# A sort loop on one core: the ranks in pieces between the products, the target rows in three parts, weights and zeros issued from inside the loop

## The chip, the cores and the metric

The kernel runs on one core of a Trainium2 chip. The metric is the device time of one execution in microseconds (us). The kernel before was run 14 times: median 19117.52 us, lowest 19084.45, highest 19168.0. The core has a matrix engine (PE), a vector engine (DVE), a scalar engine (ACT), GpSimd (POOL) and SyncE (SP), which here issues transfers (DMAs). Each runs its own list of instructions in order, and they meet at semaphores.

## The reference

A graph with 12500 nodes (16 features each) and 412500 directed edges, the edges ordered by `dst`, passes through four graph layers, each added to `x`. What the changed part of the kernel does is the edge half of layer 0, for all edges:

```
h   = maximum(layernorm(x), 0)
x_j = h[dst]                                             # 412500 rows
m   = silu(einsum('ei,ej,ijh->eh', x_j, edge_attr_8, W_msg_tp) / sqrt(16 * 8))
m   = m @ W_msg_lin / sqrt(16)
agg = segment_sum(m, src, num_segments=12500)
...                                                      # node update, then x = x + ...
```

Layers 1 to 3 (a weighted message layer, an encoder with two edge and node blocks, two graph convolutions) use the same edges in the order into which layer 0's stage has sorted them. Of them only the loading of their weights is touched.

## The kernel before

The nodes are padded to 12544 = 98 windows of 128 (`ND`). The edges of a window (by `dst`) lie together in the input, so a window is a stretch of 35 x 128 edge records (`TL` = 35) of 16 words. Within its window every edge gets a slot by the group of its source node: a table of 37 x 128 slots (`TT` = 37; the last 5 of the 37 columns take what overflows), kept in DRAM as `cells`. From the slots, messages can be computed with one-hot matrix products and without address lists.

**Before the loop.** `tile_gnn` first builds constants, then loads all weights of the four layers with SP and prepares them on DVE: L188 to L288, with the helpers `load_w` (L114), `load_b` (L119), `center` (L124), `pair_diag` (L131), `bias_rows` (L144) and `twice` (L232). SP then loads `X`, and ten DMAs from one large tile of zeros (L322 to L327) clear the sum tables in DRAM. `relu_ln` (L729, called at L1600) forms H = relu(layernorm(X)), and `table128` (L988) forms a table `t_msg` of 128 numbers for each node. `sort_edges` (L366) begins with `window_starts` (L335), which counts on DVE where each window's edges begin; a sum over partitions on POOL ends it.

**The loop** (L413 to L466) runs 98 + 5 times; an iteration serves windows of different age. It is written under a manual schedule for PE, DVE, ACT and SP: the engines' lists have the order of the program text. The pieces of the `Window` class (L478), with the age at which a window meets them:

- `load` (age -1; SP): clears the window's slots in DRAM and loads its edge records `rec`.
- `keys` (age 0; DVE, L498 to L513): source group of each edge. `hot_cells` (L516, L518): the one-hot rows `s_ohs` of these groups, 128 x 4480 numbers. `count` (L520 to L527; PE): 36 matmuls that count edges by group.
- `look_up` (age 1; DVE): ten small operations from the counts (L535 to L545), then one multiply (L547) and one reduction (L548) over 128 x 4480 numbers, then `s_eq`, the comparison of all edges of a partition with one another in two parts (L554 to L558). `rank` (L561 to L593): 25 small operations that end in `s_row`, the row of each edge in the table. `scatter` (L595; POOL): 35 indirect DMAs (L597) of 128 records each.
- `read_back` (age 3; SP): loads the window's slots as `c`. `slot_rows` (age 3; PE L613, ACT L615 and L616): transposes the slot numbers and writes them to `slot_lo`.
- `load_rows` (age 4; SP, L618 to L622): loads `u` from `slot_lo` and `win` from `t_msg`. `hot_rows` (age 4; ACT, L624 to L632): the one-hot rows `hot_dt` of the target nodes in three parts (`PARTS`: 16, 16 and 5 columns; three buffers).
- age 5 (`old`): `gather(i)` (PE, L641), for ten chunks (`CHUNKS`, nine of 4 columns and one of 1), one-hot matmuls into one of two PSUM banks `pl`, two records in the profile for each matmul; `products(i)` (DVE, L650), their product with the edge features; `message(i)` (DVE L662, ACT), the reduction of a part of the columns and silu; `hot_sources` (DVE, L656), one-hot rows of the source nodes; `to_sources` (PE, L675), 32 matmuls (64 records) that add the messages into the accumulators `acc`.

PE, DVE and POOL are bound together: `rank` follows on `count` of the iteration before, `scatter` on `rank`, `products` on `gather`, and `gather(i + 2)` must wait for `products(i)`, because there are two `pl` banks. `slot_rows` takes a `pl` bank too. In the code before, an iteration issues, after the loads, `look_up`, `rank` and `scatter` of the window of age 1 first, and then the gathers, products and the rest in the order of the text printed here.

Of the kernel before, what the change touches and what calls it, by code (L numbers as in the profile page):

```python
# [11 lines left out]
F32 = mybir.dt.float32  # L12
# [35 lines left out]
def tile_gnn(ctx: ExitStack, tc: tile.TileContext, a: dict, out: bass.AP):  # L48
# [82 lines left out]
    def pair_diag(name, src, centered):  # L131

        d = consts.tile([P, P], F32, name=name)
        two = consts.tile([P, 64], F32, name=name + "_2")
        v.memset(d, 0.0)
        sp.dma_start(two[0:64, :], src)
        sp.dma_start(two[64:128, :], src)
        if centered:
            center(two, 64)
        v.tensor_copy(d[0:64, 0:64], two[0:64, :])  # L140
        v.tensor_copy(d[64:128, 64:128], two[64:128, :])
        return d

    def bias_rows(name, src, centered):  # L144

        b = consts.tile([3, 64], F32, name=name + "_f")
        sp.dma_start(b, row_bc(src, 64, 3))
        if centered:
            center(b, 64)
        part = consts.tile([3, 3, 64], BF16, name=name + "_p")  # L150
        back = consts.tile([3, 64], F32, name=name + "_b")
        acc = consts.tile([3, 64], F32, name=name + "_a")
        for k in range(3):
            v.tensor_copy(part[:, k, :], b)
            v.tensor_copy(back, part[:, k, :])
            v.tensor_sub(b, b, back)
            if k == 0:
                v.tensor_scalar(acc, back, ident[0:3, 0:1], None, op0=ALU.mult)
            else:
                v.scalar_tensor_tensor(acc, back, ident[0:3, k:k + 1], acc, op0=ALU.mult, op1=ALU.add)  # L160
        r = consts.tile([P, 8, 64], BF16, name=name)
        v.memset(r, 0.0)
        v.tensor_copy(r[0:3], acc[:, None, :].to_broadcast([3, 8, 64]))
        return r.rearrange("p t f -> p (t f)")
# [27 lines left out]
    wml = load_w("wml", a["L0_gnn_W_msg_lin"], 16, 16)  # L192
    v.tensor_scalar(wml, wml, 0.25, None, op0=ALU.mult)
    wupd = load_w("wupd", a["L0_gnn_W_upd_tp"].rearrange("i h k -> i (h k)"), 16, 256)
    v.tensor_scalar(wupd, wupd, 1.0 / 16.0, None, op0=ALU.mult)
    wul = load_w("wul", a["L0_gnn_W_upd_lin"], 16, 16)
    v.tensor_scalar(wul, wul, 0.25, None, op0=ALU.mult)
    w1t = load_w("w1t", a["L1_w_iao"], 16, 128)
    w1c = consts.tile([P, 16], F32, name="w1c")
    for j in range(8):  # L200
        sp.dma_start(w1c[16 * j:16 * j + 16, :], a["L1_w_iao"][:, 16 * j:16 * j + 16])
    b1_l1 = load_b("b1_l1", a["L1_gnn_bias"], 16)

    p2 = "L2_gnn_"
    ne_w0 = load_w("ne_w0", a[p2 + "node_enc_w0"], 16, 64)
    ne_b0 = load_b("ne_b0", a[p2 + "node_enc_b0"], 64)
    ne_w1 = load_w("ne_w1", a[p2 + "node_enc_w1"], 64, 64)
    center(ne_w1, 64)
    ne_b1 = load_b("ne_b1", a[p2 + "node_enc_b1"], 64)
    center(ne_b1, 64)  # L210
    ne_g = load_b("ne_g", a[p2 + "node_enc_g"], 64)
    ne_be = load_b("ne_be", a[p2 + "node_enc_beta"], 64)

    ee_w0 = consts.tile([P, 8, 64], F32, name="ee_w0")
    v.memset(ee_w0, 0.0)
    for t in range(TS):
        sp.dma_start(ee_w0[8 * t:8 * t + 8, t % 8, :], a[p2 + "edge_enc_w0"])
    ee_w0 = ee_w0.rearrange("p t f -> p (t f)")

    ec_w0 = consts.tile([P, 8, 64], F32, name="ec_w0")  # L220
    v.memset(ec_w0, 0.0)
    for t in range(8):
        sp.dma_start(ec_w0[WORDS * t:WORDS * t + 8, t, :], a[p2 + "edge_enc_w0"])
        sp.dma_start(ec_w0[WORDS * t + W_ONE:WORDS * t + W_ONE + 1, t, :], row_bc(a[p2 + "edge_enc_b0"], 64, 1))
    ec_w0 = ec_w0.rearrange("p t f -> p (t f)")
    ee_b0 = bias_rows("ee_b0", a[p2 + "edge_enc_b0"], False)
    ee_w1 = pair_diag("ee_w1", a[p2 + "edge_enc_w1"], True)
    ee_b1 = bias_rows("ee_b1", a[p2 + "edge_enc_b1"], True)
    ee_g = load_b("ee_g", a[p2 + "edge_enc_g"], 64)
    ee_be = load_b("ee_be", a[p2 + "edge_enc_beta"], 64)  # L230
# [8 lines left out]
    ee_g2 = twice("ee_g2", a[p2 + "edge_enc_g"])  # L239
    ee_be2 = twice("ee_be2", a[p2 + "edge_enc_beta"])  # L240

    eb, nb = [], []
    for s in range(2):
        w0, f = a[p2 + "edge_blk_w0"][s], {}
        f["w0e"] = pair_diag(f"eb_w0e{s}", w0[0:64, :], False)
        f["w0sd"] = consts.tile([64, 128], F32, name=f"eb_w0sd{s}")
        sp.dma_start(f["w0sd"][:, 0:64], w0[64:128, :])
        sp.dma_start(f["w0sd"][:, 64:128], w0[128:192, :])
        f["b0"] = load_b(f"eb_b0{s}", a[p2 + "edge_blk_b0"][s], 64)
        f["w1"] = pair_diag(f"eb_w1{s}", a[p2 + "edge_blk_w1"][s], True)  # L250
        f["w1x"] = consts.tile([P, P], F32, name=f"eb_w1x{s}")
        v.memset(f["w1x"], 0.0)
        sp.dma_start(f["w1x"][0:64, 64:128], f["w1"][64:128, 64:128])
        sp.dma_start(f["w1x"][64:128, 0:64], f["w1"][0:64, 0:64])
        f["b1"] = bias_rows(f"eb_b1{s}", a[p2 + "edge_blk_b1"][s], True)
        f["g"] = load_b(f"eb_g{s}", a[p2 + "edge_blk_g"][s], 64)
        f["be"] = load_b(f"eb_be{s}", a[p2 + "edge_blk_beta"][s], 64)
        f["g2"] = twice(f"eb_g2{s}", a[p2 + "edge_blk_g"][s])
        eb.append(f)
        f = {}  # L260
        f["w0"] = load_w(f"nb_w0{s}", a[p2 + "node_blk_w0"][s], 128, 64)
        f["b0"] = load_b(f"nb_b0{s}", a[p2 + "node_blk_b0"][s], 64)
        f["w1"] = load_w(f"nb_w1{s}", a[p2 + "node_blk_w1"][s], 64, 64)
        center(f["w1"], 64)
        f["b1"] = load_b(f"nb_b1{s}", a[p2 + "node_blk_b1"][s], 64)
        center(f["b1"], 64)
        f["g"] = load_b(f"nb_g{s}", a[p2 + "node_blk_g"][s], 64)
        f["be"] = load_b(f"nb_be{s}", a[p2 + "node_blk_beta"][s], 64)
        nb.append(f)

    eb[0]["sum_be"], eb[1]["sum_be"] = consts.tile([P, 64], F32, name="sum_be"), eb[1]["be"]
    v.tensor_add(eb[0]["sum_be"], eb[0]["be"], ee_be)

    be0 = twice("eb_be2", a[p2 + "edge_blk_beta"][0])
    be_w0e = consts.tile([P, 64], F32, name="be_w0e")
    with banks(**usual):
        pb0 = bank("pa")
        pe.matmul(pb0[:, 0:64], lhsT=be0[0:64, :].to_broadcast([64, P]), rhs=eb[1]["w0e"][0:64, 0:64], start=True,
                  stop=True)
        v.tensor_copy(be_w0e, pb0[:, 0:64])  # L280
    dec_w0 = load_w("dec_w0", a[p2 + "dec_w0"], 64, 64)
    dec_b0 = load_b("dec_b0", a[p2 + "dec_b0"], 64)
    dec_w1 = load_w("dec_w1", a[p2 + "dec_w1"], 64, 16)
    dec_b1 = load_b("dec_b1", a[p2 + "dec_b1"], 16)
    gw1 = load_w("gw1", a["L3_w1_t"], 16, 32)
    gb1 = load_b("gb1", a["L3_gnn_b1"], 32)
    gw2 = load_w("gw2", a["L3_w2_t"], 32, 16)
    gb2 = load_b("gb2", a["L3_gnn_b2"], 16)  # L288
# [33 lines left out]
    sp.dma_start(X, a["x"].rearrange("(p c) d -> p c d", c=C))  # L322
    with tc.tile_pool(name="prep", bufs=1) as wk:
        zero = wk.tile([P, (C + 1) * 64], F32, name="zero")
        v.memset(zero, 0.0)
        for t in [*g_l0, g_l1, *g_l2, *g_gc, t_acc]:
            sp.dma_start(t.rearrange("(p c) d -> p (c d)", p=P), zero[:, :t.shape[0] // P * t.shape[1]])  # L327
# [7 lines left out]
    def window_starts(wk):  # L335
# [4 lines left out]
        sp.dma_start(di, a["dst"].rearrange("(p j) -> p j", p=P))  # L340
        v.tensor_single_scalar(di, di, 7, op=ALU.arith_shift_right)
# [24 lines left out]
    def sort_edges():  # L366


        with tc.tile_pool(name="ws", bufs=1) as wk:
            window_starts(wk)  # L370
        with tc.tile_pool(name="so1", bufs=1) as one, tc.tile_pool(name="so", bufs=2) as ed, \
# [38 lines left out]
            with tc.manual_schedule(engines={et.PE, et.DVE, et.Activation, et.SP}):  # L410
                ws = [Window(g, k, ed) for g in range(ND)]
                ws[0].load()
                for g in range(ND + LAG):  # L413
                    def at(lag):
                        return [ws[g - lag]] if 0 <= g - lag < ND else []
# [6 lines left out]
                    for w in at(1):  # L422
                        w.look_up()
                        w.rank()
                        w.scatter()
                    old, new = at(LAG), at(0)
                    for w in old:
                        w.gather(0)
                        w.gather(1)
                        w.products(0)  # L430
                        w.gather(2)
                        w.products(1)
                        w.gather(3)
                    for w in new:
                        w.keys()
# [1369 lines left out]
```

## Time and profile before

| what | us |
|---|---|
| median of 14 runs (lowest, highest) | 19117.52 (19084.45, 19168.0) |
| the profiled execution | 19101.04 |
| its span | 19099.3 |
| first scatter of the sort loop starts at | 214.2 |
| sort loop ends at about | 7207 |
| PE, DVE, ACT, POOL busy over the span | 12860.3, 12479.8, 6082.3, 6999.9 |
| POOL's scatters: number, mean | 3430, 0.958 |

The profile is one execution of the program, with the start and duration of every instruction. A group of instructions is shown as line, engine, operation, tiles (written <- read), count, then after the bar the total busy time in us and the mean in ns, and after the second bar the idle time of that engine just before these instructions, with what ended most of it. "remote" and "issue" there mean that the profile shows no instruction of another engine that ended the wait. In a timeline, each line is a start, a duration, the engine, the line of the code, the operation, and in square brackets the idle time before it. In a table of windows each engine has its busy time in that stretch and the number of its instructions; PEclk is the granted clock of PE as a share of full speed.

### The profile page before, as it was taken

Reading aid. Unit: us, or ns where it says so; the run is one execution under the profiler, and the core shown is the slowest. Engines: PE = TensorE matmul, PEld = TensorE weight load, DVE = VectorE, ACT = ScalarE, POOL = GpSimd, SP = SyncE. Lnnn points to the kernel's source line nnn. Section 1 sums busy time; section 2 is a strip of 40 time slices with the busy share of each in tenths; the row PEclk is TensorE's granted clock in tenths of the full one; section 3 lists DMA queues with packets and bytes.
Section 4 is the critical chain, followed back from the end, with each engine's and each line's share of the span. In section 5 each row is a group of like instructions: output and inputs, shape, how many; then the busy total and the mean of one; then the engine's idle time right before and its main releaser. Section 6 shows DMA issues by size and latency. Waiting matters only on the chain. (4 is left out here: it accounts for less than half of the span.)

```text
span 19099.3 us, 387064 instructions
## 1 busy us (share of the span) xinstructions
PE 12860.3 (67%) x161327; PEld 10282.6 (54%) x161327; DVE 12479.8 (65%) x23622; ACT 6082.3 (32%) x10025; POOL 6999.9 (37%) x6387
## 2 busy tenths in 40 slices
PE   1444444444444448999788688888879999756666
PEld 1444433444344346777577666666656666644444
DVE  5555555555555556777788677777757777655555
ACT  0111111111111125555377522222223333234343
POOL 3444444444444442333245311111113322144444
PEclk6666666666666669999899899999989999866666
DMA  1101010100001004444366544444433434266666
GB/s 67 28 25 28 28 28 25 28 28 27 26 28 28 25 24 106 126 125 126 106 172 175 141 130 135 136 136 136 136 109 117 119 112 117 72 169 175 164 177 169
DMA packets 1361577, 1827.92 MB, mean 96 GB/s; under 512 B 501594, under 2 KB 794970, under 8 KB 1358526
## 3 DMA queue, kind: packets, MB, share of 16 engines
q1 hardware_dynamic: 1079624, 1721.34, 29.7%
q0 software_dynamic: 258720, 76.68, 4.1%
q8 instruction: 1275, 20.89, 0.5%
q10 hardware_dynamic: 21462, 4.95, 0.1%
q14 instruction: 496, 4.06, 0.1%
HBM read 1296.64 MB, written 504.92 MB: 94 GB/s over the span
## 5 line engine op out<-in xcount | busy, mean ns | idle before, releaser
L597 POOL DMA_INDIRECT cells<-rec,s_row x3430 | 3285.2, 958 | 3636.0 <-DVE s_row L593 2530.2
L1467 POOL DMA_INDIRECT xo<-t_src,c x980 | 1243.6, 1269 | 4425.2 <-DMA c<-cells 2396.3
L641 PE MATMUL pl<-win,hot_dt 128*128 128x128 f32 x7252 | 1429.8, 370 | 2128.5 <-DVE wide L650 1642.1
L641 PEld LDWEIGHTS pl<-win,hot_dt 128*128 128x128 f32 x7252 | 1330.5, 279 | 2186.5 <-DVE wide L650 1676.2
L650 DVE TENSOR_TENSOR wide<-pl,c 128x512 f32<-128x512 f32 x980 | 603.0, 645 | 2706.5 <-remote 2517.4
L675 PE MATMUL acc<-parted,hot_s 128*98 128x64 f32 x6272 | 1175.4, 339 | 1663.8 <-issue 1657.3
L675 PEld LDWEIGHTS acc<-parted,hot_s 128*98 128x98 f32 x6272 | 1081.9, 260 | 1780.8 <-issue 1770.8
L1221 ACT ACTIVATE sq<-po 128x512 f32<-128x512 f32 (+1 forms) x1470 | 831.2, 565 | 3686.7 <-PE po L1218 2830.1
L1273 PE MATMUL pa<-hot,y 128*64 128x128 f32 x21756 | 1671.8, 284 | 241.2 <-issue 157.3
L1224 DVE TENSOR_REDUCE nsum<-sq 128x8 f32<-128x512 f32 (+1 forms) x1470 | 945.5, 643 | 1137.3 <-ACT sq L1221 1023.1
L1011 POOL DMA_INDIRECT xo<-t_gc,c x980 | 1033.8, 1055 | 1588.7 <-DMA c<-cells 549.6
L1238 DVE TENSOR_TENSOR hot<-iota_row,lod 128x512 f32<-128x512 f32 x2352 | 1514.1, 685 | 0.0
L1273 PEld LDWEIGHTS pa<-hot,y 128*64 128x64 f32 x21756 | 1209.6, 138 | 529.5 <-issue 336.4
L812 POOL DMA_INDIRECT g_l<-summed,row x490 | 803.5, 1640 | 1459.0 <-ACT summed L808 1134.9
L666 ACT ACTIVATE parted<-pre 32x256 f32<-32x256 f32 x784 | 324.4, 414 | 3178.2 <-issue 2367.2
L1082 DVE TENSOR_REDUCE x<-po 128x128 f32<-128x384 f32 x1176 | 650.0, 553 | 1036.9 <-remote 484.7
L1514 PE MATMUL po<-hot_dt,td 128*64 128x256 f32 (+2 forms) x7056 | 1013.1, 404 | 8.0 <-DVE hot_dt L1490 8.0
L631 ACT ACTIVATE hot_dt<-off,one_col 128x2048 f32<-128x2048 bf16 (+1 forms) x294 | 473.4, 1610 | 1652.7 <-remote 1614.4
L1059 ACT ACTIVATE off<-places,minus_col 98x1024 bf16<-98x1024 uint8 x784 | 897.5, 1145 | 271.4 <-DMA places<-slot_lo 194.5
L1209 ACT ACTIVATE hidn<-po 128x512 f32<-128x512 f32 (+1 forms) x1470 | 857.1, 583 | 332.1 <-PE po L1514 273.0
L1514 PEld LDWEIGHTS po<-hot_st,tab 98*64 98x64 f32 x25088 | 879.6, 138 | 137.3 <-issue 22.7
L1233 DVE TENSOR_TENSOR y<-y,nr 128x512 f32<-128x512 f32 (+1 forms) x1470 | 946.8, 644 | 5.1
(380 smaller groups left out, 27709.5 us busy)
## 6 DMA issues: line engine op xcount, KB each, us to landing
hot_dk<-keep_t SPq DMA_DIRECT2D x588, 512.0 KB
e_feat<-ft SPq DMA_DIRECT2D x882, 256.0 KB
ft<-e_feat SPq DMA_DIRECT2D x882, 256.0 KB
c<-cells SPq DMA_DIRECT2D x392, 296.0 KB
keep_t<-hot SPq DMA_DIRECT2D x392, 256.0 KB
ud<-slot_lo SPq DMA_DIRECT2D x98, 1024.0 KB
c<-cells SPq DMA_DIRECT2D x147, 592.0 KB
us<-slot_lo SPq DMA_DIRECT2D x98, 784.0 KB
```

What stands on the lines that cost most here:

```text
L597: ins = gp.indirect_dma_start(out=self.cells, out_offset=bass.IndirectOffsetOnAxis(ap=self.row[:, t:t + 1], axis=0), in_=self.rec[:, t, :] ...
L641: pe.matmul(pl[:, t * P:(t + 1) * P], lhsT=self.hots[t0 // 16][:, o:o + P], rhs=self.win, start=True, stop=True, skip_group_check=True)
L675: pe.matmul(acc[t // 8][0:C, o:o + 64], lhsT=self.hot[:, t, :], rhs=self.k["parted"][self.g % 2][:, t, :, :].rearrange("p q f -> p (q f)") ...
L1011: gp.indirect_dma_start(out=out[:, t, :], out_offset=None, in_=table, in_offset=bass.IndirectOffsetOnAxis(ap=c[:, TC + t, W_SRC:W_SRC + 1] ...
L1059: sc.activation(off, u, AF.Abs, bias=minus_col[:C, :])
L1209: sc.activation(self.hid[:, :n], po[:, :n], AF.Silu)
L1224: return lambda: v.tensor_reduce(self.sums[:, 8 * c:8 * c + 2 * k], sq[:, :2 * k, :], AX.X, ALU.add)
L1233: v.tensor_tensor(w, w, bc_last(self.r[:, 8 * c:8 * c + 2 * k], 64), ALU.mult)
L1238: v.tensor_tensor(hot[:, w].rearrange("p (h t) d -> p h t d", h=2), iota_row[:, None, None, :].to_broadcast([P, 2, 2, P]), lo[:, :, :, Non ...
L1273: pe.matmul(self.acc[64 * w:64 * w + 64, 0:P], lhsT=lhsT, rhs=rhs, start=c == 0 and i < 2, stop=c == 9 and i >= len(work) - 2, skip_group_ ...
L1467: gp.indirect_dma_start(out=self.xo[:, w, t, :], out_offset=None, in_=t_src[s], in_offset=bass.IndirectOffsetOnAxis(ap=self.c[:, w, TC + t ...
L1514: pe.matmul(out[o:o + 64], lhsT=lhsT, rhs=rhs, start=start, stop=stop, skip_group_check=True)
```

## The change

*Prologue.* Before the sort, only `W_msg_tp` is loaded and prepared. `window_starts` runs first, and its `ws_di` load goes ahead of the load of `X`; then `relu_ln`, `table128` and the sort follow. All other weights, the zeros and their small DVE operations move into a generator `weights(zero)`, with a `yield` after each small group: memsets, loads, 41 DMAs of zeros from a smaller tile (128 x 784 numbers, so 401 KB at most each), copies and centerings. The loop takes one step of it per iteration, from the second on. The matmul for `be_w0e` comes after the sort.

*Loop.* `look_up` keeps its ten small operations. L547 and L548 become `spread(0)` and `spread(1)` (18 and 17 of the 35 columns; a tile `s_hit` of their own instead of `wide`); the comparisons become `same_cell(0)` and `same_cell(1)`. `hot_rows` takes the part as an argument. `gather(i + 2)` is issued right behind `products(i)`, and the first two gathers of a window at the end of the iteration before, ahead of that iteration's `to_sources`. The iteration's new order:

```diff
                 ws[0].load()
+                zero = one.tile([P, C * 8], F32, name="zero")
+                v.memset(zero, 0.0)
+                others = weights(zero)
                 for g in range(ND + LAG):
+                    if g:
+                        next(others, None)
...
+                    prev, old, new, then = at(1), at(LAG), at(0), at(LAG - 1)
+                    def products(i):
+                        for w in old:
+                            w.products(i)
+                            if i + 2 < len(CHUNKS):
+                                w.gather(i + 2)
+                    for w in prev:
                         w.look_up()
-                        w.rank()
-                        w.scatter()
+                    products(0)
+                    for w in prev:
+                        w.spread(0)
+                    products(1)
+                    for w in prev:
+                        w.spread(1)
+                    products(2)
+                    for w in prev:
+                        w.same_cell(0)
+                    products(3)
+                    for w in old:
+                        w.message(0)
+                    for w in prev:
+                        w.same_cell(1)
+                    products(4)
+                    for w in then:
+                        w.hot_rows(0)
+                    for w in prev:
+                        w.rank()
+                        w.scatter()
+                    products(5)
+                    for w in new:
+                        w.keys()
+                        w.hot_cells()
+                        w.count()
+                    products(6)
+                    for w in old:
+                        w.hot_sources()
+                    products(7)
+                    for w in old:
+                        w.message(1)
+                    for w in then:
+                        w.hot_rows(1)
+                    products(8)
+                    for w in at(LAG - 2):
+                        w.slot_rows()
+                    products(9)
+                    for w in old:
+                        w.message(2)
+                    for w in then:
+                        w.hot_rows(2)
+                        w.gather(0)
+                        w.gather(1)
                     for w in old:
                         w.to_sources(acc)
-                    for w in at(LAG - 2):
-                        w.slot_rows()
+                for _ in others:
+                    pass
```

The generator, cut to its kinds of steps:

```diff
+    def weights(zero):
...
+        ec_w0 = consts.tile([P, 8, 64], F32, name="ec_w0")
+        v.memset(ec_w0, 0.0)
+        yield
...
+        for name, src, centered in pairs:
...
+            sp.dma_start(two[0:64, :], src)
+            sp.dma_start(two[64:128, :], src)
+            diags[name] = (d, two, centered)
+            yield
...
+        n = zero.shape[1]
+        for t in [*g_l0, g_l1, *g_l2, *g_gc, t_acc]:
+            w = t.shape[0] // P * t.shape[1]
+            for o in range(0, w, n):
+                k = min(n, w - o)
+                sp.dma_start(t.rearrange("(p c) d -> p (c d)", p=P)[:, o:o + k], zero[:, :k])
+                yield
+        for name, (d, two, centered) in diags.items():
+            if centered:
+                center(two, 64)
+                yield
...
```

The two new functions of the window:

```diff
+        def spread(self, part):
+            t0, t1 = (0, TL // 2 + 1) if part == 0 else (TL // 2 + 1, TL)
+            hit = self.ed.tile([P, TL // 2 + 1, P], F32, name="s_hit", bufs=1)[:, :t1 - t0, :]
+            v.tensor_tensor(hit, self.ohs[:, t0:t1, :], bc_mid(self.k["pc"][:, P:2 * P], t1 - t0), ALU.mult)
+            v.tensor_reduce(self.both[:, t0:t1], hit, AX.X, ALU.add)
...
+        def same_cell(self, part):
+            if part == 0:
+                self.eq, self.pre = self.ed.tile([P, TL, TL], F32, name="s_eq", bufs=1), self.small("s_pre")
...
+            e, n = self.eq[:, t0:t1, 0:t1], t1 - t0
...
+            if part == 1:
+                v.tensor_add(self.both, self.both, pre)
```

## The prediction

> **What bounds the kernel now.** The diff touches the prologue and the sort loop, which end at about 7207 us; nothing after that changes but one small matmul. I read the costliest groups first, then the waits of DVE in the loop, then the timeline of one period, then a table of short windows.
>
> ```profile
> L597 POOL DMA_INDIRECT cells<-rec,s_row x3430 | 3285.2, 958 | 3636.0 <-DVE s_row L593 2530.2
> L650 DVE TENSOR_TENSOR wide<-pl,c 128x512 f32<-128x512 f32 x980 | 603.0, 645 | 2706.5 <-remote 2517.4
> L675 PE MATMUL acc<-parted,hot_s 128*98 128x64 f32 x6272 | 1175.4, 339 | 1663.8 <-issue 1657.3
> ```
>
> POOL issues 35 scatters per window, each 0.958 us and 0.30 us of pause (44.2 us for 35), and then waits for the next ranks, `s_row`: 2530 us over 97 gaps, 26 to 27 us each. No engine is full. One period on the timeline (POOL, DVE and PE rows):
>
> ```profile
> 3576.81 0.96 POOL L597 DMA_INDIRECT cells<-rec,s_row  x1 [26.54 <-DVE s_row L593]
> ...
> 3619.74 0.96 POOL L597 DMA_INDIRECT cells<-rec,s_row  x1 [0.30 <-issue]
> 3647.89 0.95 POOL L597 DMA_INDIRECT cells<-rec,s_row  x1 [27.19 <-DVE s_row L593]
> ```
> ```profile
> 3624.72 0.89 DVE L650 TENSOR_TENSOR wide<-pl,c 128x512 f32<-128x512 f32 x2 [27.88 <-remote]
> ```
> ```profile
> 3624.00 0.26 PE L675 MATMUL acc<-parted,hot_s 128*98 128x64 f32 x1 [1.13 <-issue]
> 3624.70 6.27 PE L675 MATMUL acc<-parted,hot_s 128*98 128x64 f32 x37 [0.44 <-issue]
> ```
>
> DVE waits 27.9 us for products(8), whose gather's records ended long before, and is let go 47.9 us after the first scatter, about 4 us after the last. At the same moment PE, which had been issuing single matmuls 0.7 to 2.8 us apart, runs 37 records in 6.27 us. The windows show this crawl:
>
> ```profile
> core 0: us, PE busy (x) PEld busy (x) DVE busy (x) ACT busy (x) POOL busy (x), PEclk, DMA share, GB/s
> 226.00:249.00 23.00, 1.05 (x11) 0.84 (x9) 20.06 (x44) 0.00 (x0) 17.51 (x19) 0.63 0.04 7
> 249.00:259.00 10.00, 0.00 (x0) 0.00 (x0) 2.03 (x12) 0.00 (x0) 7.56 (x9) 0.50 0.04 7
> ...
> 3600.00:3612.00 12.00, 2.57 (x11) 1.85 (x10) 0.00 (x0) 7.21 (x5) 9.12 (x10) 0.69 0.04 6
> 3612.00:3624.00 12.00, 1.59 (x7) 1.66 (x7) 0.00 (x0) 0.00 (x0) 6.71 (x7) 0.50 0.03 6
> 3625.00:3631.00 6.00, 6.00 (x38) 5.97 (x38) 5.58 (x14) 0.93 (x2) 0.00 (x0) 0.50 0.03 7
> ```
>
> From some 20 us into a scatter until it is over the other engines get few instructions through; at 249 us it strikes DVE too. No view names its cause; I use it as a fact with a place and an end. So the period is 47.9 us (scatter and crawl) plus 23.2 us of DVE until the next scatter: products(8,9) and message(2) 1.7, look_up's small operations 2.9, L547 and L548 9.7, the comparisons (`s_eq`, with the add) 3.8, rank 4.85, 0.28 to POOL. 47.9 + 23.2 = 71.1, also the mean over the 92 periods from 521.3 to 7062.0 us.
>
> **The change, part by part.**
>
> *Prologue.* The first scatter starts at 214.2 us. The weights' loads and small operations end at 55.4 us, and then
>
> ```profile
> DVE ln_s L733 <- DMA t_acc<-zero: 37.1, 1, 37.1
> ```
>
> X is waited for behind 13 MB of zeros. Both go: 55.4 + 37.1 = 92. Window_starts moves ahead of relu_ln and the table; its own wait for `ws_di` (1.5 + 6.6 us) stays. I take -92 us (80 to 100). The be_w0e matmul comes after the sort, +1 us.
>
> *Weights in the loop.* About 102 small pieces, one at each iteration's start: on DVE a memset or a few copies (a centering is three rows of 0.14 to 0.3 us), on SP at most 401 KB of zeros. DVE meets them ahead of look_up, where it will later wait for PE (next), so they are hidden; without that cover they cost 0.5 us x 40 = 20 us. On SP they stand behind the window's loads.
>
> *Loop order.* At the iteration's start now stand look_up and products(0) to (4) with spread (L547/L548 in two halves), the comparisons and message(0) between; then rank and scatter; then products(5), keys, hot_cells, count, hot_sources, products(6) to (9) and messages. With t = 0 at the first scatter, DVE does: products(5) 0.65, keys 2.1, hot_cells 4.8, products(6) 0.65, hot_sources 3.4, products(7) 0.65, message(1) 2.3, together 14.6; products(8) once count (36 records) and gather(8) are through, about 16; products(9), message(2) to 17.5; look_up to 20.4, products(0) 21. Spread (4 x 2.4 us) with products(1) follows, by 32 us even if a few of these six operations crawl. All of it lies beside the scatter's 44.2 us: that is the gain. That such DVE work runs there at full length, and POOL keeps its step, the early row 226:249 shows: it holds look_up, L547, L548, the comparisons and rank of window 1, 20.06 us in 23, with 19 scatters.
>
> But products(2) needs gather(2), and that stands on PE behind to_sources of the window before (64 records, L675). The code puts two gathers of the next window ahead of to_sources; both take the bank that products(9) and then products(0) free, so to_sources starts at about 22 us, inside the crawl. What is left of it at 47.9 us now delays DVE, where before nothing waited for it. How much is left is the uncertain size. By records passed: until 47.9 us PE passed 121 records before (29 gather matmuls of 2 records, count 36, to_sources 27); now it must pass 136 (gathers 34, transposes 2, count 36, to_sources 64), and DVE about 12 more operations, so some 21 records are left, 3.5 us at 6.27/37 = 0.169. By the crawl's own speed (18 in 24 us, rows 3600 to 3624), 46 are left, 7.8 us. The bounds are 0 and 7.8; before left 37 (6.3 us). I take 30 records, 5.1 us, between the two readings.
>
> Then gather(2), 8 records, 1.2 us, and DVE's chain to the scatter: products(2) 0.65, comparisons 1.46, products(3) 0.65, message(0) 2.29, comparisons and add 2.33, products(4) 0.65, rank 4.85, 0.28: 13.2. Gathers 3 and 4 (1.2 us each) hide behind the comparisons and message(0). Period: 47.9 + 5.1 + 1.2 + 13.2 = **67.4 us** (62.3 to 70.1), 3.7 less than 71.1; 92 x 3.7 = 340 (92 to 810). The first and last iterations, without that chain, I count at nothing.
>
> Sum against the profiled execution's 19,101.0 us: 19,101 - 92 - 340 + 1 = 18,670. The median of the 14 runs is 16 us above the profiled one, so for a median I say **18,685 us** (forecast's own range 18,210 to 18,930).
>
> The scatters read SBUF beside DVE for longer now. [...]
>
> **Rivals.**
>
> 1. *The crawl eases.* If the crawl hangs on how PE and DVE work is spread, to_sources and the gathers get through by about 35 us, the chain of 13.2 runs within the scatter, and the period falls to DVE's work (42.7 us busy) with its waits for gathers, 50 to 60 us: 19,101 - 92 - 92 x 11..21 = 17,080 to 18,000. For: back-to-back scatters were done at 214 and 258 us. Against: the scatter at 7061.5, with no new window beside it, still crawled to its end. 0.11.
> 2. *DVE is caught too* (slower). If DVE's small operations pass the crawl at the 12 in 10 us of row 249:259 or less, with count or gather(8) late, look_up is only begun when the crawl ends. Then 47.9 + 2.9 + 0.65 + 9.7 + 0.65 + 13.2 = 75.0: 19,101 - 92 + 92 x 3.9 = 19,370. It decides from 72.1 us on, where the loop's loss eats the 92 us. Against: DVE has done 17.5 us of work before the place where the crawl began (20 to 35 us). 0.13.
> 3. *SP's loads fall into the scatter.* slot_rows now ends at about 17 us, so the burst (u 592, empty and c 296, rec 280 KB, with 401 KB of zeros) lies beside scatter packets and may end the crawl 4 to 6 us later: about 71 to 73 us, 19,010 to 19,190. Against: after the scatter at 258 to 303 us, with loads beside it, DVE was let go 8.6 us after its end, and 8.9 after the next pair. 0.12, over all signs.
> 4. *Only the prologue moves*; the loop's gain goes into the wait for to_sources: 19,010. 0.02.
> 5. *POOL and DVE exclude each other*: were each spread operation to hold the scatter for its length, 9.6 us, the period would be 77 us, 19,550. The row 226:249 speaks against it: 0.02. [...]
>
> **Numbers.** Forecast 0.60; rivals 0.11, 0.13, 0.12, 0.02, 0.02. About 0.2% (38 us) is what a measurement of this kernel can tell from no change. Faster: 0.60 + 0.11 + 0.02 and 0.05 of rival 3 = 0.78; same: 0.04 of rival 3; slower: 0.13 + 0.02 + 0.03 = 0.18. The range 18,000 to 19,200 takes in the forecast's bounds, rivals 3 and 4 and the near part of 2, and leaves out rival 1, the far part of 2 and rival 5, about 0.2.
>
> **What would show it.** Right: first scatter at about 122 us; scatters 67 us apart; POOL's idle time per gap down from 26.5 to 23; DVE's long wait now before products(2) (L650, released by PE), with look_up and spread done inside the scatter; L675 still crawling. Wrong: DVE's long wait still before look_up (rival 2), the crawl's end later than 48 us after the first scatter (3), L675 running at 0.17 us a record inside the scatter (1), or L597 longer than 0.96 us beside L547's successor (5).

## The result and the profile after

The changed kernel took 18875.18 us (median of 6 runs, 18847.46 to 18893.75), the kernel before 19119.65 (28 runs): ratio 0.9872, 95% interval 0.9862 to 0.9882, so 244 us less. Forecast were 434 us less, 18,685.

| profiled executions, us | before | after | difference |
|---|---|---|---|
| time | 19101.04 | 18837.17 | -263.9 |
| first scatter starts | 214.2 | 122.2 | -92.0 |
| first to last window's scatter (97 periods) | 6847.8 | 6709.0 | -138.8 |
| mean period, from the ninth window on | 71.08 | 69.52 | -1.56 |
| last window's scatter to the end of the last accumulation | 145.6 | 159.6 | +14 |
| the rest of the program | 11,892 | 11,845 | -47 |

The first scatter's 92.0 us and the 138.8 of the 97 periods are the change; the +14 lies in the loop's last iterations, whose order is new too. The last row is noise of the later stages, whose code is the same but for one small matmul: in a second profile of the changed kernel (e5, below) the rest took 11,912, 67 more than here.

The three groups that were shown of before, on the page of the changed kernel (L652, L706 and L731 are the lines that were L597, L650 and L675):

```profile
L652 POOL DMA_INDIRECT cells<-rec,s_row x3430 | 3299.6, 962 | 3483.0 <-DVE s_row L648 2380.7
...
L706 DVE TENSOR_TENSOR wide<-pl,c 128x512 f32<-128x512 f32 x980 | 631.3, 646 | 2509.3 <-remote 1943.4
...
L731 PE MATMUL acc<-parted,hot_s 128*98 128x64 f32 x6272 | 1056.5, 352 | 750.4 <-issue 749.4
```

POOL still waits 2381 us for the ranks, only 150 less than before. DVE's waits without a named releaser went from 2517 to 1943 us. One period, as the timelines of POOL, DVE and PE show it:

```profile
3492.24 0.96 POOL L652 DMA_INDIRECT cells<-rec,s_row  x1 [25.38 <-DVE s_row L648]
...
3535.28 0.96 POOL L652 DMA_INDIRECT cells<-rec,s_row  x1 [0.30 <-issue]
3561.97 0.96 POOL L652 DMA_INDIRECT cells<-rec,s_row  x1 [25.73 <-DVE s_row L648]
```
```profile
3511.15 0.89 DVE L706 TENSOR_TENSOR wide<-pl,c 128x512 f32<-128x512 f32 x2 [4.63 <-remote]
...
3515.47 0.29 DVE L592 TENSOR_TENSOR pc<-s_run,po 128x128 f32<-128x128 f32 x1
3531.61 0.69 DVE L706 TENSOR_TENSOR wide<-pl,c 128x512 f32<-128x512 f32 x1 [15.85 <-remote]
...
3540.76 0.69 DVE L706 TENSOR_TENSOR wide<-pl,c 128x512 f32<-128x512 f32 x1 [3.41 <-remote]
...
3548.97 0.69 DVE L706 TENSOR_TENSOR wide<-pl,c 128x512 f32<-128x512 f32 x1 [2.74 <-PE pl L697]
...
3561.51 0.18 DVE L648 TENSOR_SCALAR s_row<-s_inc 128x35 int32<-128x35 f32 x1 [0.21 <-DVE s_inc L646]
```
```profile
3534.22 4.48 PE L731 MATMUL acc<-parted,hot_s 128*98 128x64 f32 x26
3539.99 0.27 PE L731 MATMUL acc<-parted,hot_s 128*98 128x64 f32 x1 [1.29 <-issue]
3540.70 6.42 PE L731 MATMUL acc<-parted,hot_s 128*98 128x64 f32 x37 [0.44 <-issue]
3546.91 3.97 PE L697 MATMUL pl<-win,hot_dt 128*128 128x128 f32 x24
```

Read them against the clock of the scatter (first issue at 3492.24, last at 3535.28). Look_up is done 23.5 us after the first issue. The one long wait of before has become four: products(8) at 3511.15, products(0) at 3531.61, products(1) at 3540.76, let go when the crawl ends 48.5 us after the first issue, and products(2) at 3548.97, the only one whose releaser is named: gather(2), behind the 37 records of to_sources that PE runs from 3540.70 on. (The 26 records before them ran at the same pace, 0.17 us each, once products(0) and gather(1) were through; then PE was held again until 3540.70.) From products(2) the chain of the ranks takes 13.0 us to the next scatter.

### The profile page after: what moved, and what is told of

Read it like the earlier page. It is cut to its first block, busy times and chain, and to the rows that moved or that the text cites. A ratio compares the mean times of both kernels' runs of the same rounds, so it can differ in the third digit from the quotient of the medians.

```text
span 18835.4 us, 387280 instructions
## 1 busy us (share of the span) xinstructions
PE 12893.3 (68%) x161327; PEld 10259.7 (54%) x161327; DVE 12526.0 (67%) x23818; ACT 6101.3 (32%) x10025; POOL 7064.8 (38%) x6387
## 5 line engine op out<-in xcount | busy, mean ns | idle before, releaser
L652 POOL DMA_INDIRECT cells<-rec,s_row x3430 | 3299.6, 962 | 3483.0 <-DVE s_row L648 2380.7
L706 DVE TENSOR_TENSOR wide<-pl,c 128x512 f32<-128x512 f32 x980 | 631.3, 646 | 2509.3 <-remote 1943.4
L731 PE MATMUL acc<-parted,hot_s 128*98 128x64 f32 x6272 | 1056.5, 352 | 750.4 <-issue 749.4
L731 PEld LDWEIGHTS acc<-parted,hot_s 128*98 128x98 f32 x6272 | 1035.2, 272 | 773.4 <-issue 772.6
L1138 DVE TENSOR_REDUCE x<-po 128x128 f32<-128x384 f32 x1176 | 650.9, 553 | 983.7 <-PE po L1129 400.4
L1147 DVE TENSOR_TENSOR hot_d<-iota_row,c 128x1024 f32<-128x1024 f32 (+1 forms) x882 | 949.1, 1076 | 0.0
```

The lines of the kernel that those rows point to most:

```text
L652: ins = gp.indirect_dma_start(out=self.cells, out_offset=bass.IndirectOffsetOnAxis(ap=self.row[:, t:t + 1], axis=0), in_=self.rec[:, t, :] ...
L731: pe.matmul(acc[t // 8][0:C, o:o + 64], lhsT=self.hot[:, t, :], rhs=self.k["parted"][self.g % 2][:, t, :, :].rearrange("p q f -> p (q f)") ...
L1147: v.tensor_tensor(o[:, :k, :], bc_mid(iota_row, k), bc_last(self.c[:, t0:t0 + k, W_LD], P), ALU.is_equal)
```

## The experiments

Each ratio is to the kernel before, run beside it on the same chip. The groups met different conditions, and no number below can be read without them: in the first comparison and in the groups of e1 to e4 and e5 to e7 the kernel before took 19,120, 19,364 and 19,113 us; in the last two (e8 to e10, e11 and e12) the same kernel took 15,571 and 15,561.

### e1: the order of before, with the new prologue

The iteration's text of before is put back, `look_up`, `spread`, `same_cell`, `rank`, `scatter` first; the prologue and `weights` stay.

> The changed kernel with the loop order of before (ranks ahead of everything, gathers, products and to_sources as before); the prologue and the weights in the loop stay. If the prologue gives 92 us and the loop order the rest of the 244, the time is about 19,028 us and the scatters are 71.1 us apart. If loading weights and zeros in the loop costs something, the scatters stand further apart than 71.1 in the first hundred windows and the time is 19,050 or more. If the loop order gave nothing and the prologue everything, it is 18,875.

Measured: 19323.67 us beside 19363.65, ratio 0.9983 (0.9974 to 0.9993), 40 us less. On this chip the 92 us alone would be 0.9952. So the new order is worth about 0.9983 - 0.9872 = 1.1%, some 210 us, by a comparison of two groups of runs. The loop of e1 has lost 52 of the 92 us, and the traces show where. The weights in the loop are not free under the old order: a piece on DVE stands between message(2) and look_up, behind the crawl, as here the cast of L148:

```profile
5718.55 0.82 DVE L721 TENSOR_REDUCE pre<-wide 128x80 f32<-128x640 f32 x1
5719.29 0.40 DVE L148 CAST ee_b<-ee_b_a 3x512 bf16<-3x512 f32 x1
5719.62 0.27 DVE L585 COPY s_num<-po 128x128 f32<-128x128 f32 x1
```

From one to the other it takes 0.74 us without a piece and 1.07 to 1.50 with one, 17 us over the last 31 windows. The split multiplies and reductions take 9.97 us a window where L547 and L548 took 9.59, 36 us in all. Together that is about the 52 us, which the interval gives only to 18 us either way. The periods alone (72.57 us while the pieces are zeros, which are SP's alone, and 73.17 later) would not show it: those of the kernel before, without any piece, rise too in these stretches, from 70.9 to 71.2. In the changed kernel they are 69.45 and 69.61: hidden, as forecast.

### e2: the ranks early

The order is again that of before, but the ranks of a window come in its own iteration, behind message(1) (shortened):

```diff
                     for w in old:  # ... products(6), products(7), message(1)
+                    for w in new:
+                        w.look_up() ... w.rank(); w.scatter()
                     for w in then:
                         w.hot_rows(0); w.hot_rows(1); w.hot_rows(2)
```

> As e1, but look_up, spread, the comparisons, rank and scatter of a window stand behind message(1) of the same iteration, straight behind the count, so that this chain of DVE work (21 us) needs nothing from PE while the scatter before it runs. Theory: what the crawl holds up is chiefly DVE waiting for PE, so the ranks are ready at about 45 us, the wait of POOL shrinks from 25 to a few us, and the period is 50 to 60 us: 17,700 to 18,100 us. Rival: the crawl also passes rank's 25 small operations at about 0.8 per us, or holds the count's release; then the ranks come only after the crawl's end at 48.7 us, the period is 66 to 71 us and the time 18,600 to 19,030.

Measured: 19476.44, ratio 1.0054 (1.0038 to 1.0070); period 74.17 us. The theory fell, and the rival was too mild. DVE on the timeline, with the scatter's first issue at 3476.20:

```profile
3494.56 0.69 DVE L709 TENSOR_TENSOR wide<-pl,c 128x512 f32<-128x512 f32 x1 [0.75 <-remote]
3503.72 0.69 DVE L709 TENSOR_TENSOR wide<-pl,c 128x512 f32<-128x512 f32 x1 [8.47 <-remote]
...
3523.35 0.69 DVE L709 TENSOR_TENSOR wide<-pl,c 128x512 f32<-128x512 f32 x1 [15.60 <-remote]
...
3549.88 0.18 DVE L651 TENSOR_SCALAR s_row<-s_inc 128x35 int32<-128x35 f32 x1 [0.21 <-DVE s_inc L649]
```

With the ranks at the end, products(5) to (7) and the count fall into the crawl, the products each held by its gather, and all of look_up, spread, comparisons and ranks, 21.5 us from 3528.53 on, comes after it.

### e3: to_sources one iteration later

```diff
                     products(4)
+                    for w in at(LAG + 1):
+                        w.to_sources(acc)
...
-                    for w in old:
-                        w.to_sources(acc)
```

> The changed kernel, with to_sources of a window one iteration later, behind products(4), so that gather(2) no longer stands behind it on PE. Theory: the 37 records left at the crawl's end cost about 2 to 5 us of the period (gather(2) is waited for 2.7 us, spread(1) of 4.9 hides the rest); products(1) is still held until 48.7 us, so the period falls from 69.5 to about 67 us and the time to about 18,650. Rival A: the crawl begins after a certain number of instructions; with 64 records fewer ahead of it products(1) and spread(1) get through before it and the period falls to 55 to 62 us, 17,900 to 18,300. Rival B: to_sources was not on the path: 18,875.

Measured: 19831.56, ratio 1.0244 (1.0227 to 1.0261); period 78.39 us. All three expectations failed. PE and DVE, scatter from 3483.62:

```profile
3480.49 6.45 PE L731 MATMUL acc<-parted,hot_s 128*98 128x64 f32 x64
...
3496.56 0.27 PE L574 MATMUL po<-s_ohs,ones_bf 128*128 128x256 bf16 x1 [0.16 <-issue]
...
3518.36 0.37 PE L697 MATMUL pl<-win,hot_dt 128*128 128x128 f32 x1 [1.73 <-issue]
```
```profile
3533.26 0.89 DVE L706 TENSOR_TENSOR wide<-pl,c 128x512 f32<-128x512 f32 x2 [35.37 <-remote]
```

To_sources runs without a pause (0.10 us a record), but its end lies in the first 3 us of the scatter; the crawl then begins 12.9 us after the first issue, in the middle of the count, and catches gather(8). DVE waits 35 us for products(8), and the whole order behind it, spread included, comes after the crawl. So e3 does not price gather(2) behind to_sources: what it may have saved there is buried, for the PE work moved to the scatter's start is paid for by what it pushes into the crawl.

### e4: every second scatter left out

```diff
-            for t in range(TL):
+            for t in range(0, TL, 2):
```

> The changed kernel with every second scatter left out (18 of 35 per window, so half of the edges are not placed). Theory: the crawl lives as long as the scatter and some 4 us more: it ends at about 27 us, most of the order is then free of it, and the period is that of DVE's work and its waits for the gathers, 46 to 54 us. Rival: the crawl belongs to the other engines' own work (PE's accumulation, the clock) and not to the scatter: the period stays at 65 to 69.5 us.

Measured: 17301.12, ratio 0.8935 (0.8914 to 0.8955); period 52.0 us. DVE's "remote" waits in the sort loop fall from 1943 us to 488:

```profile
DVE wide L706 <- remote: 487.8, 113, 7.6
```

The crawl follows the scatter. It still begins some 15 us after the first issue, but in one period of its trace it lets products(0) go 24.9 us after that issue and 2.4 us after the last scatter's end. With 35 scatters products(1) was held until 48.5 us, 4.5 after the last one's end.

### e5, e6, e7: scatters further apart

e5 is the changed kernel again (0.9875, 0.9839 to 0.9910). In e6 POOL does one memset of 128 x 128 numbers behind each scatter, in e7 three, and POOL joins the manual schedule:

```diff
                 tc.add_to_no_dep_group("scattered", ins)
+                gp.memset(self.k["pace"], 0.0)
```

> The changed kernel itself, beside the next two on one chip, so that its period and its stages can be compared with theirs. Ratio to the kernel before as at first, 0.987; scatters 69.5 us apart if this chip is as the first one, more if it is slower in all stages.

> The changed kernel with one small memset on POOL (128 x 128 numbers, 0.2 us in the prologue) between two scatters, and POOL's list kept in the order of the text. Scatters then come about 1.5 us apart instead of 1.263, 52 us for 35. Theory: each scatter occupies something shared for about 1.39 us (the crawl ended 48.7 us after the first of 35 and 25 us after the first of 18), so at 1.263 us a backlog builds that after some 15 us holds up the other engines; at 1.5 us none builds, the crawl is gone, and the period is that of DVE's work with the waits for gathers or of the scatters, 52 to 58 us: ratio 0.91 to 0.94. Rival: the crawl belongs to the scatters whatever their spacing; then it lasts about 8 us longer and the period is about 77 us: ratio 1.02 to 1.03.

> As e6 with three memsets between two scatters: about 1.9 us apart, 66 us for 35. Theory: no crawl, the scatter itself is the bound, period 66 to 70 us, ratio 0.975 to 0.99, and DVE waits for POOL's buffers or not at all. Rival: the crawl stays and ends 4 us after the last scatter, period 66 + 4 + 20 = 90 us, ratio 1.09.

| | e5 | e6 | e7 |
|---|---|---|---|
| from scatter to scatter, us | 1.263 | 1.352 | 1.873 |
| first to last scatter's end, us | 43.9 | 47.1 | 65.4 |
| period, us | 69.58 | 69.46 | 66.72 |
| time, us (beside 19113.23) | 18865.48 | 18825.94 | 18604.64 |
| ratio (interval) | 0.9875 (0.9839 to 0.9910) | 0.9857 (0.9818 to 0.9897) | 0.9745 (0.9705 to 0.9786) |

DVE's longest waits in the sort loop (us in total, times, longest), for e5 and then e7:

```profile
DVE wide L706 <- remote: 1922.7, 261, 18.5
DVE wide L706 <- PE pl L697: 244.2, 92, 4.2
DVE wide L706 <- issue: 203.3, 14, 17.1
```
```profile
DVE wide L709 <- PE pl L700: 1815.4, 182, 36.8
DVE wide L709 <- issue: 440.3, 47, 30.5
```

In e7 no wait is "remote" any more (440 us without a releaser stay, under "issue"), and PE is not held late in the scatter: 68 records, 0.16 us each, in the 11 us from 3538 on, 44 us after the first issue. The crawl is gone although the scatters last 21 us longer, and POOL is the bound (1.4 us from the last scatter to the next window's first). In e6, whose spacing came out at 1.35 instead of 1.5 us, the crawl stays, though DVE's "remote" waits fall to 1532 us, and the time is that of e5. So a spacing of 1.873 us removes the crawl, and POOL's place in the schedule, which e6 shares, does not. The point of 1.39 us is not shown, since it lies between the two spacings tried.

### e8 to e12: the same questions where the kernel before takes 15,570 us

e8 has two memsets (1.61 us), e9 and e12 memsets of 128 and 48 columns (1.53 us), e10 is the kernel before with the pacing of e8, e11 the changed kernel.

> The changed kernel with two memsets of 128 x 128 between two scatters and POOL's list in the order of the text: about 1.61 us from scatter to scatter (1.35 with one, 1.87 with three), 56 us for 35. Theory (each scatter takes something shared for about 1.39 us; only a closer spacing builds a backlog): no wait of DVE without a releaser, POOL is the bound, period 57 us, 12 less than the 69.6 of the changed kernel: ratio to the kernel before 0.920 to 0.930. Rival (the crawl goes only with much wider spacing, or comes with any scatter after some 20 us): period 66 to 75 us, ratio 0.97 to 1.01.

> As e8 with memsets of 128 x 128 and 128 x 48: about 1.54 us from scatter to scatter, 54 us for 35. Theory: still above 1.39, no crawl, period 54 to 56 us or DVE's own round of about 50: ratio 0.905 to 0.915. Rival: the point lies between 1.54 and 1.61 or above, and the period is 66 to 70 us.

> The kernel before, order and prologue unchanged, with the pacing of e8. If the crawl is what set the period in the order of before too, and 1.61 us removes it, the period is that of the scatter (57 us) or of DVE's round (42.7 us of work and its waits for gathers, about 50): ratio 0.930 to 0.940, the prologue's 92 us above e8. Then the order of the loop is worth nothing once the crawl is gone. If the old order has a bound of its own (DVE's 23 us of ranks between two scatters), the period is 56 + 23 = 79 us: ratio 1.04.

> The changed kernel once more, beside e12. If the kernel before takes about 19,100 us here (crawl present), 0.987 as in the first two comparisons. If it takes about 15,570 us as in the last group (no crawl), theory: the loop of both orders is bound by the 35 scatters and the hand-over to the next (45 to 46 us), the order is worth nothing and only the prologue's 92 us are left: ratio 0.994, about 15,480 us. Rival: without the crawl the new order's two chains, gather(2) behind to_sources and 13 us of ranks behind it, make DVE's round longer than the scatter, 50 us or more: ratio 1.02 or more.

> The kernel of e9 (scatters 1.53 us apart) again, beside the changed kernel itself. With the crawl present (before at about 19,100 us), theory of the shared 1.39 us: no crawl at 1.53 us, period 55 us, ratio 0.91 to 0.92; rival: crawl as in e6 (1.35 us apart), period 69 to 70 us, ratio 0.985. Without the crawl (before at about 15,570 us): the pacing alone bounds the period, 54.8 us as in e9, ratio 1.057.

| | e8 | e9 | e10 | e11 | e12 |
|---|---|---|---|---|---|
| period, us | 57.32 | 54.84 | 57.32 | 47.35 | 54.84 |
| time, us | 16720.80 | 16465.86 | 16824.17 | 15745.48 | 16489.79 |
| ratio | 1.0730 | 1.0574 | 1.0801 | 1.0115 | 1.0599 |
| interval | 1.0711 to 1.0748 | 1.0555 to 1.0592 | 1.0783 to 1.0819 | 1.0091 to 1.0140 | 1.0576 to 1.0622 |

No trace of these groups has a crawl, whatever the spacing (among DVE's longest waits in the loops of e8 to e11 none is "remote"), so e8, e9 and e12 could not find the point where it starts; their expectations for a present crawl stay untested. Two things they show. With POOL as the bound, the order is worth nothing: e10 is 103 us above e8, about the prologue's 92. And without the crawl the changed kernel is the slower one, e11, by 0.9 to 1.4%: the rival of its expectation, at about half the size that it gave. POOL, DVE and PE there:

```profile
2504.86 0.96 POOL L652 DMA_INDIRECT cells<-rec,s_row  x1 [3.46 <-DVE s_row L648]
```
```profile
2539.51 0.69 DVE L706 TENSOR_TENSOR wide<-pl,c 128x512 f32<-128x512 f32 x1 [4.16 <-PE pl L697]
```
```profile
2526.84 10.81 PE L731 MATMUL acc<-parted,hot_s 128*98 128x64 f32 x64
```

Products(2) waits 4.16 us for gather(2), which stands behind the 10.81 us of to_sources (granted clock 0.50 there), and POOL waits 3.46 us for the ranks: the round of DVE, 47.8 us (median), is the bound, where the scatter alone is 44.2. Without the 4.16 us the round would be 43.6, so gather(2) is what makes it the bound; that is worked out from these rows, and no run takes the wait away. The kernel before has no trace in this condition; from its time, 92 us of prologue more and 184.5 us in all less, its period must be (92 + 184.5) / 97 = 2.9 us shorter, 44.5, about the scatter's own. The trace of e10, the same kernel but for the pacing, says nearly the same: 214 us before the first scatter, 119 behind the last window's and 10,944 of rest leave 44.2 us for each of 97 periods. Both are inferred.

None of these kernels was best in both conditions: among those that place all edges, e7 is the fastest where the crawl is present, the kernel before where it is not. E7 was not run there; e8, with scatters closer together, was already 7.3% slower.

## Why the prediction held, and where its sum was off

The change gained 244 of the 434 us that were forecast: the bound and the prologue were right, the length of the period was not.

*What bounds the kernel.* The chain of scatter, crawl and DVE's work behind it was the bound: e4 shortens the crawl and e7 removes it, and the "remote" waits fall from some 1930 us to 488 and to none.

*Prologue, -92.* Measured -92.0 at the first scatter.

*Weights in the loop, hidden.* Right: 69.45 to 69.61 us. E1 shows their price where the cover is gone, 17 us; the prediction had said 20.

*Work beside the scatter.* Right for look_up, which ends 22.9 us after the first issue (medians of the periods here and below; forecast 20.4). The rest failed. Products(0) was let go at 38.6 us, not 21, so DVE's long wait stood before it, not before products(2); spread(0) ended at 44.3, with the scatter itself (44.0); and products(1), to be passed by 32, was held until 48.4. That this added nothing to the period is luck: products(1) and spread(1), 5.5 us that the sum does not have behind the crawl, fitted into the 8.1 us until PE let products(2) go.

*The period.* Forecast 47.9 + 5.1 + 1.2 + 13.2 = 67.4; measured, by medians, 48.4 to products(1), 8.1 from there to products(2), and 13.0 to the scatter, 69.5. The steps that failed are the two in the middle, "I take 30 records, 5.1 us" and "gather(2), 8 records, 1.2 us". 37 records were left (6.4 us), and the gather and its hand-over took 1.7. The reading that counted records until the crawl's end (21 left) was wrong, and not for want of a start in time: in 22 of 87 periods to_sources began some 23 us after the first issue, as forecast, in the others some 40, and 35 to 39 records were left either way. The nearest row, before's own 37, was the answer; that is luck in part, since 35 to 63 were left in the periods of before. 2.1 us over 92 windows is 193 us; the median missed the forecast by 190.

*Rivals.* The first, an easier crawl, and the third, a later end, did not happen: the crawl ended 48.4 us after the first issue, 0.5 later than the forecast had it. The second happened in part: gathers rather than DVE's small operations were caught, and products(0) and (1) with them. The fourth fell, as the loop gained 138.8 us, and so did the fifth: the scatters beside spread's multiplies took 0.961 us, the others 0.962.

*What the sum could not see.* The order's worth hangs on the crawl. The same step that was mis-sized, gather(2) behind to_sources, is the wait in e11, where there is no crawl and the changed kernel is 1.15% slower.

## What to carry to other kernels

A wait that no instruction of the profile ends, on several engines at once, is a condition to be tested before an order is built around it: thin out or space the work it runs beside, and run the kernel before again at another time and on another chip. Where PE passes few instructions for a stretch, what counts is which of them stand ahead of the ones DVE waits for; in e3, moving work out of one queue position pushed other work in, and products(8) was held for 35.4 us. If a new order puts a gather behind a long accumulation, price that wait as if the rest were perfect: here its 4.16 us remained when the stall was gone.

## What the runs showed of the hardware that was not expected

The crawl comes beside the scatters, but not in every condition: the same kernel before ran in 19,113 to 19,364 us with it and in 15,561 to 15,571 without. One chip by its number had both, 19,364 in the group of e1 and 15,571 in that of e8. The difference is not the sort loop's alone: the rest of the program took 10,897 to 10,944 us in e8 to e12 and 11,845 to 12,059 in all other traces, that of e7 included, whose sort loop has no crawl. There too the longer stages have waits on several engines that no instruction ends: in the changed kernel's trace 389 us on DVE before L1138 and 357 on ACT before L1645, with no wait of that kind in the trace of e11.

Beside the crawl the traces also hold fewer records of the semaphore steps of landing DMAs. In the trace of e11, without the crawl, most stretches of 5 us of the scatter hold 64, in which four scatters are issued, so 16 for each, and the whole trace 198,091. That of the first profile after, with the crawl, holds 108,038 for the same program, and between 25 and 45 us after the first issue 5 to 9 in 5 us (medians here and below). In e7, at 1.873 us, it is 32 to 49 from 10 us on, about the full 43, and there is no crawl. The scatters' packets themselves are not late: in the crawl they end 1.7 us after the issue in most cases, as without it. The records thin out before the instructions do: in the changed kernel there are 64 records in the stretch from 5 to 10 us and 17, 12 and 4 in the next three, while PE, DVE and ACT still start 19 instructions from 20 to 25 us and none, by the median, from 25 to 35. No run here shows whether the missing records have to do with the cause, and whether the crawl would be there in an execution without a record cannot be told from these traces; the times with and without a profile agree, 18837.17 beside a median of 18875.18. When the crawl starts is open too: it began 35 us after the first issue in the first scatter of before, 22.8 in one in its middle and 12.9 in e3, with 156, 258 and 186 instructions (weight loads counted) passed since that issue, so neither after a fixed time nor after a fixed count.
